# Attention over a graph's edges: the fifth chunk of slots of each group of sources becomes one chunk shared by four groups, scored once per block

## The chip, the cores and the metric

The kernel runs on one core of one Trainium2 chip. The metric is the device time of one launch in microseconds. Fourteen runs of the kernel before gave a median of 10038.4 us, from 10018.83 to 10051.82.

## The reference

The input is a graph of 10,000 nodes (512 features each) and 160,000 edges `src`, `dst` with eight attention biases per edge. Layer 0 is a mixture of four two-layer SAGE experts with a norm. Layer 1, which the change touches, is attention over the edges of each source:

```python
s = jnp.einsum('ehd,ehd->eh', q[src], k[dst]) / np.sqrt(D) + att_bias
m = jax.ops.segment_max(s, src, num_segments=n)
p = jnp.exp(s - m[src])
denom = jax.ops.segment_sum(p, src, num_segments=n)
alpha = p / jnp.where(denom[src] == 0, 1.0, denom[src])
agg = jax.ops.segment_sum(alpha[:, :, None] * v[dst], src, num_segments=n)
att = agg.reshape(n, C) @ Wo.T + bo
```

A residual, a norm and an MLP with `silu` (512 to 1024 to 512) follow, and a norm ends the layer.

## The kernel before

**Groups and slots.** The 10,112 padded nodes are 79 blocks of 128, and each block is four groups of 32 nodes (`W`=32, `NQ`=4), 316 groups in all (`NW`). A group has on average 506 edges. For layer 1 each group of sources owns five chunks (`CAP`=5) of 128 slots, 640 slots, in a table `sorted1` of ten floats per slot: the index of `dst`, the place of the source in its group, the eight biases. Empty slots carry an index out of bounds, which a gather skips. `fail` sends the launch to a slow general path if some group has more edges than slots.

**Three stages.** Stage 1 (to about 4000 us) and stage 2 (to about 7000 us) compute layer 0 and q, k, v, and TensorE is busy nearly throughout. Beside stage 1, `plan_src` works out each edge's slot on VectorE. It is a generator that `side(e, f)` drives from the loop of stage 1: four steps per call while it counts, then one. When it is done, `scatter_src` writes the edges to their slots, 128 per indirect DMA, 1250 DMAs: 28 per pair of blocks for the rest of stage 1, and seven per block in stage 2. Any that are left are issued at the end of stage 2.

**Stage 3** is the attention and the MLP, one loop iteration per group `w` (block `b`, `j = w % 4`). The order of instructions on TensorE (PE), VectorE (DVE), ScalarE (ACT) and GpSimd (POOL) is the order of the code. The attention of a group is spread over four iterations by the generator `weigh`. In iteration `w`:

1. `advance(EARLY)` issues MLP or output matmuls of earlier blocks (jobs `front`, `back`, `tail`) worth about 2.6 us of PE, with the ACT and DVE steps that belong to them.
2. `score(0)`: DVE multiplies two chunks of gathered k by the queries that PE has spread to the slots, in PSUM (`qe`, L1709). `score(1)` takes chunks 2 and 3, and `score(2)` the fifth chunk alone. `expand(w, g)` (L1695) makes `qe`: one matmul per chunk from the turned one-hots. There are two `qe` buffers, so `expand(w, 2)` waits for `score(0)`, `expand(w+1, 0)` for `score(1)`, `expand(w+1, 1)` for `score(2)`.
3. Between these, for group `w-1`: DVE takes a maximum (L1605), PE spreads it (L1607), DVE subtracts it (L1609), ACT takes the exponential (L1612), POOL and DVE multiply it into the one-hots (L1621). For `w-2`: PE adds up 80 small matmuls (L1635).
4. `pull(w+2)`: POOL issues the five gathers of k and v rows (L1476) into one of four buffers. The first is `ring`, which serves the groups with `j = 0`.
5. `turn_hots(w+2)`: PE turns five one-hots (L1485) into a PSUM bank named `turns`, and ACT copies them out (L1488). The bank `turns` holds the outputs of L1485, L1602 and L1607.
6. `advance(LATE)` issues job work worth about 2.4 us of PE. In it, ACT may have a Silu (L1545) of an MLP slice that PE has just made (L1543), or the normed rows (L1515), or a copy (L1527).
7. DVE sums the products over each head (L1736, five chunks at once), adds the bias (L1738), and takes the maximum over the chunks (L1600). PE turns that (L1602), and all later PE work stands behind it. Then come DVE's reciprocal (L1640, L1641) and ACT's scaling (L1644) for `w-2`.

The lines of step 7:

```python
s = dp.tile([P, CAP, H], F32, name="s")
nc.vector.tensor_reduce(s, kv[:, :, :D].rearrange("p c (h d) -> p c h d", h=H), axis=AX.X, op=ALU.add)
nc.vector.tensor_add(s, s, blocks[b][0][:, j * CAP:(j + 1) * CAP, 2:])
first = weigh(w, s)
next(first)                 # L1600: maximum over the chunks
next(first, 1)              # L1602: PE turns it
```

At `j = 1` the loop opens block `b+2`: it loads the slots and makes the one-hots (L1450 on DVE, L1452 on ACT).

Of the kernel before, what the change touches and what calls it, by code (L numbers as in the profile page):

```python
# [18 lines left out]
P = 128  # L19
# [606 lines left out]
NS = len(SEQ)  # L626
ET = mybir.EngineType
# [3 lines left out]
def fast(ctx: ExitStack, tc: tile.TileContext, a: dict, out: bass.AP, bad: bass.AP):  # L631

# [14 lines left out]
    NC = NW * CAP  # L647
# [16 lines left out]
    nc.gpsimd.iota(iota_w, pattern=[[1, W]], base=0, channel_multiplier=0,  # L664
                   allow_small_or_imprecise_dtypes=True)
# [230 lines left out]
    DIG = 1024.0  # L896
    SC = max(C, 2 * D)

    def plan_src(pool, ps):
        src_i = pool.tile([P, SC], I32, name="scan")[:, :C]  # L900
        nc.sync.dma_start(src_i, a["src"].rearrange("(p c) -> p c", c=C))
        pair = pool.tile([P, SC], BF16, name="pair")[:, :C]
        digit = pool.tile([P, C], BF16, name="digit")
        nc.vector.tensor_single_scalar(addr_i, src_i, 6, op=ALU.logical_shift_right)
        nc.vector.tensor_copy(pair, addr_i)
        nc.vector.tensor_scalar(addr_i, src_i, 5, 1, op0=ALU.logical_shift_right,
                                op1=ALU.bitwise_and)
        nc.vector.tensor_scalar(digit, addr_i, DIG - 1.0, 1.0, op0=ALU.mult, op1=ALU.add)
        yield
        count = pool.tile([P, NPR], F32, name="count")  # L910
        for b in range(NPR):
            m = pool.tile([P, C], BF16, name="m")
            nc.vector.scalar_tensor_tensor(m, pair, float(b), digit, op0=ALU.is_equal,  # L913
                                           op1=ALU.mult, accum_out=count[:, b:b + 1])
            yield
        num_i = pool.tile([P, NPR], I32, name="num_i")
        dig_i = pool.tile([P, NPR], I32, name="dig_i")
        nc.vector.tensor_copy(num_i, count)
        num = pool.tile([P, NPR, 2], F32, name="num")
        nc.vector.tensor_single_scalar(dig_i, num_i, 1023, op=ALU.bitwise_and)  # L920
        nc.vector.tensor_copy(num[:, :, 0], dig_i)
        nc.vector.tensor_single_scalar(dig_i, num_i, 10, op=ALU.logical_shift_right)
        nc.vector.tensor_copy(num[:, :, 1], dig_i)
        upper = pool.tile([P, P], F32, name="upper")
        nc.gpsimd.iota(upper, pattern=[[1, P]], base=0, channel_multiplier=-1,
                       allow_small_or_imprecise_dtypes=True)
        nc.vector.tensor_scalar(upper, upper, 0.0, None, op0=ALU.is_gt)
        flat = num.rearrange("p b q -> p (b q)")
        total = ps.tile([P, 512], F32, name="mm")
        nc.tensor.matmul(total[:, :NW], ones, flat, start=True, stop=True)  # L930
        top = pool.tile([P, 2], F32, name="top")
        nc.vector.tensor_reduce(top[:, 0:1], total[:, :NW], axis=AX.X, op=ALU.max)
        nc.vector.tensor_reduce(top[:, 1:2], total[:, :NW], axis=AX.X, op=ALU.add)
        nc.vector.tensor_scalar(fail[:, 1:2], top[:, 0:1], float(SL), None, op0=ALU.is_gt)
        nc.vector.tensor_scalar(fail[:, 2:3], top[:, 1:2], float(E), None, op0=ALU.not_equal)
        first = ps.tile([P, 512], F32, name="mm")
        nc.tensor.matmul(first[:, :NW], upper, flat, start=True, stop=True)
        two = first[:, :NW].rearrange("p (b q) -> p b q", q=2)
        nc.vector.tensor_copy(num, two)
        nc.vector.scalar_tensor_tensor(count, num[:, :, 1], DIG, num[:, :, 0],  # L940
                                       op0=ALU.mult, op1=ALU.add)
        nc.vector.memset(addr, 0.0)
        yield
        one = ones[:, 0:1].to_broadcast([P, C])
        for b in range(NPR):
            m = pool.tile([P, C], BF16, name="m")
            nc.vector.scalar_tensor_tensor(m, pair, float(b), digit, op0=ALU.is_equal,
                                           op1=ALU.mult)
            s = pool.tile([P, SC], F32, name="scan")[:, :C]
            nc.vector.tensor_tensor_scan(s, one, m, count[:, b:b + 1], op0=ALU.mult, op1=ALU.add)  # L950
            nc.vector.copy_predicated(addr, m.bitcast(mybir.dt.int16), s)
            yield

        nc.vector.tensor_sub(addr, addr, digit)
        rank = pool.tile([P, SC], I32, name="scan")[:, :C]
        nc.vector.tensor_copy(rank, addr)
        nc.vector.tensor_scalar(digit, digit, 1.0, 10.0 / (DIG - 1.0), op0=ALU.subtract,
                                op1=ALU.mult)
        nc.vector.tensor_copy(addr_i, digit)
        nc.vector.tensor_tensor(rank, rank, addr_i, op=ALU.logical_shift_right)  # L960
        yield
        nc.vector.tensor_scalar(digit, digit, 0.1, None, op0=ALU.mult)
        nc.vector.scalar_tensor_tensor(addr, pair, 2.0, digit, op0=ALU.mult, op1=ALU.add)
        nc.vector.tensor_scalar(addr, addr, float(CAP), None, op0=ALU.mult)
        part = pool.tile([P, C], I32, name="part")
        nc.vector.tensor_scalar(part, rank, 7, 7, op0=ALU.logical_shift_right,
                                op1=ALU.bitwise_and)
        nc.vector.tensor_add(addr, addr, part)
        nc.vector.tensor_single_scalar(part, rank, P - 1, op=ALU.bitwise_and)
        nc.vector.scalar_tensor_tensor(addr_i, part, float(NC), addr, op0=ALU.mult, op1=ALU.add)  # L970
        yield
# [3 lines left out]
    def scatter_src(pool):  # L975
# [3 lines left out]
        for c0 in range(0, C, GS):  # L979
# [6 lines left out]
            nc.vector.tensor_single_scalar(ends[:, 0, :n], ends[:, 0, :n], W - 1,  # L986
# [401 lines left out]
    with ExitStack() as p3:  # L1388
# [47 lines left out]
        kvb = [ring.rearrange("p (c v) -> p c v", c=CAP)]  # L1436
        kvb += [gp.tile([P, CAP, KVW], F32, name=f"kv{i}") for i in range(1, KB)]
# [6 lines left out]
        def open_block(b):  # L1444
            if b >= NB:
                return
            meta = dp.tile([P, BC, WP], F32, name="meta", bufs=3)
            nc.sync.dma_start(meta, slots1[:, b * BC:(b + 1) * BC, :])
            oh = dp.tile([P, BC, 3, W], BF16, name="oh", bufs=3)
            nc.vector.tensor_tensor(oh[:, :, 0, :], meta[:, :, 1:2].to_broadcast([P, BC, W]),  # L1450
                                    iota_w[:, None, :].to_broadcast([P, BC, W]), op=ALU.is_equal)
# [17 lines left out]

        def pull(w, cs):  # L1470

            if w >= NW:
                return
            b, j = divmod(w, NQ)
            for c in cs:
                nc.gpsimd.indirect_dma_start(  # L1476
                    out=kvb[w % KB][:, c, :], out_offset=None, in_=kv_all[:],
                    in_offset=bass.IndirectOffsetOnAxis(
                        ap=blocks[b][0].bitcast(I32)[:, j * CAP + c, 0:1], axis=0),
                    bounds_check=NP - 1, oob_is_err=False)  # L1480

        def turn_hots(w):
            b, j = divmod(w, NQ)
            for c in range(CAP):
                nc.tensor.transpose(hot_t[:3 * W, c, :], blocks[b][1][:, j * CAP + c, :, :]  # L1485
                                    .rearrange("p t n -> p (t n)"), identb)
            oh_t = dp.tile([3 * W, CAP, P], BF16, name="oh_t", bufs=4)
            nc.scalar.copy(oh_t, hot_t[:3 * W])  # L1488
            return oh_t
# [104 lines left out]
        def weigh(w, s):  # L1594
# [35 lines left out]
            kv = kvb[w % KB]  # L1630
            for c in range(CAP):
                for f in range(2):
                    for h in range(4):
                        v = D + (f * 4 + h) * VH
                        nc.tensor.matmul(acc[h * W:(h + 1) * W, f, :], ohp[:, c, f * 4 + h, :],  # L1635
                                         kv[:, c, v:v + VH], start=(c == 0 and f == 0),
# [38 lines left out]
        with tc.manual_schedule(engines={ET.PE, ET.DVE, ET.Activation, ET.Pool}):  # L1675
            for t in kvb[1:]:
# [3 lines left out]
            open_query(0)  # L1680
            for w in range(KB):
                pull(w, range(CAP))
            hots = {w: turn_hots(w) for w in range(2)}
            one, two, three = iter(()), iter(()), iter(())
            qe = {}

            GROUPS = [(0, 1), (2, 3), (4,)]
# [9 lines left out]

            expand(0, 0)
            expand(0, 1)
            EARLY, LATE = 2.6, 2.4  # L1700
            for w in range(NW + 3):
                b, j = divmod(w, NQ)
                kv = kvb[w % KB]

                def score(g):
                    if w < NW:
                        cs = GROUPS[g]
                        k = kv[:, cs[0]:cs[-1] + 1, :D]
                        nc.vector.tensor_tensor(k, qe.pop((w, g))[:, :len(cs), :], k, op=ALU.mult)  # L1709
# [6 lines left out]
                expand(w, 2)  # L1716
# [5 lines left out]
                expand(w + 1, 0)  # L1722
                score(2)
                next(one, 1)
                if w >= 2:
                    pull(w - 2 + KB, range(CAP))
# [4 lines left out]
                expand(w + 1, 1)  # L1731
                advance(LATE)
                first = iter(())
                if w < NW:
                    s = dp.tile([P, CAP, H], F32, name="s")
                    nc.vector.tensor_reduce(s, kv[:, :, :D].rearrange("p c (h d) -> p c h d", h=H),  # L1736
                                            axis=AX.X, op=ALU.add)
                    nc.vector.tensor_add(s, s, blocks[b][0][:, j * CAP:(j + 1) * CAP, 2:])  # L1738
# [68 lines left out]
```

## Time and profile before

| | |
|---|---|
| median of 14 runs | 10038.4 us |
| the profiled execution | 10027.07 us, of which the span is 10025.2 us |
| granted TensorE clock | 0.979 |
| busy share of the span | PE 94%, DVE 54%, POOL 71%, ACT 30% |
| loop of stage 3 | from 7038 us (first L1738) to 9928 us (last), 316 iterations |
| first and last scatter | 1488.8 us and 6888 us |

The profile is of one execution. A row of the view of groups gives a line, an engine, an operation, the tiles that it writes and reads, a count, busy time, the mean of one in nanoseconds, and the idle time of the engine before it with what ended it. The view of waits gives who waited for whom, with total, count and longest. The timeline gives start and duration of single instructions, and in brackets the idle time before them. A share over the whole span mixes three stages with different limits, so that stage 3 is read by itself.

### The profile page before, as it was taken

To read this page: it belongs to the slowest core of one execution; us is meant where nothing else is said; L and a number is where in the kernel's file an instruction comes from. 1 tells how busy PE (TensorE), PEld (TensorE's weight loads), DVE (VectorE), ACT (ScalarE), POOL (GpSimd) and SP (SyncE) were. 2 spreads that over 40 slices of the span, in tenths; PEclk is the share of its full clock that TensorE was granted. 3 is DMA by queue.
4 is the path that set the end of the run, shared out by engine and by line. 5 is a ranking of instruction groups with operands and counts; after the bars stand their busy time and mean duration, and the time that the engine had idled before them with its cause. 6 is when DMAs were issued, how large, how long until landed. Compare 5 with 4: busy or idle time off the path is not lost.

```text
span 10025.2 us, 169049 instructions
## 1 busy us (share of the span) xinstructions
PE 9441.3 (94%) x63574; PEld 5532.4 (55%) x63887; DVE 5378.4 (54%) x8205; ACT 2981.7 (30%) x5432; POOL 7126.4 (71%) x6972
## 2 busy tenths in 40 slices
PE   7999999999999998999999999999788888888888
PEld 4666666666666666333333333334455555555555
DVE  7898980000100003343343344333899999999996
ACT  1111111111111111111111111111466666666665
POOL 5566666777777774777777777775777777777774
PEclk9999999999999999999999999999799999999999
DMA  6544455455555543888888888886788888888884
GB/s 213 181 154 156 156 164 162 154 162 155 163 163 160 165 154 129 281 291 294 298 292 291 295 296 291 294 299 225 252 257 266 258 259 261 260 262 252 258 263 127
DMA packets 1110444, 2258.71 MB, mean 225 GB/s; under 512 B 284587, under 2 KB 534342, under 8 KB 1108848
## 3 DMA queue, kind: packets, MB, share of 16 engines
q0 software_dynamic: 622352, 1654.70, 51.6%
q1 hardware_dynamic: 479546, 579.42, 16.9%
q10 hardware_dynamic: 7718, 13.65, 0.4%
q8 instruction: 508, 8.32, 0.3%
q14 instruction: 320, 2.62, 0.1%
HBM read 2300.44 MB, written 380.18 MB: 267 GB/s over the span
## 4 chain that ended last, share of the span: by engine, by line
PE 68%; DVE 13%; DMA 9%; ACT 5%; issue 3%; POOL 1%; SPq 0%; POOLq 0%; ACTq 0%; DVEq 0%; another core or an unknown queue 0%
PE mm L1123 20%; PE mm L1314 11%; PE mm L1133 10%; PE mm L1276 6%; PE p_ag L1353 6%; DVE s L1736 3%; PE p_ag L1084 3%; DMA y<-y_tab,ix 3%; DMA ring<-kv_all,meta 3%; PE bank L1553 3%; DVE m L913 2%; PE bank L1503 2%; PE bank L1543 2%; DVE kv L1709 2%; ACT L1612 1%
## 5 line engine op out<-in xcount | busy, mean ns | idle before, releaser
L1059 POOL DMA_INDIRECT ring<-in_x_dram,idx_t x1580 | 1891.4, 1197 | 1006.4 <-PE p_ag L1084 559.8
L1123 PE MATMUL mm<-tt,big 128*128 128x256 f32 (+1 forms) x8960 | 1966.0, 378 | 0.0
L1123 PEld LDWEIGHTS mm<-tt,big 128*128 128x128 f32 x8960 | 1681.5, 190 | 290.5 <-issue 70.5
L993 POOL DMA_INDIRECT sorted<-pay,addr x1250 | 1270.7, 1017 | 385.4 <-issue 338.5
L1476 POOL DMA_INDIRECT kv<-kv_all,meta x1185 | 1214.6, 1025 | 330.1 <-issue 207.4
L1259 POOL DMA_INDIRECT y<-y_tab,ix x920 | 934.5, 1016 | 311.6 <-issue 189.8
L1314 PE MATMUL mm<-big,hb 128*128 128x512 f32 x2528 | 1145.9, 596 | 8.2
L1133 PE MATMUL mm<-wn,h 128*128 128x512 f32 x2528 | 1124.0, 597 | 0.0
L1125 ACT ACTIVATE h<-mm,bl 128x256 f32<-128x256 f32 (+1 forms) x640 | 301.3, 471 | 2126.8 <-PE mm L1123 2126.8
L1259 POOL DMA_INDIRECT ring<-y_tab,ix x660 | 684.8, 1038 | 292.1 <-issue 137.2
L1276 PE MATMUL mm<-big,z_t 128*128 128x512 f32 x1896 | 852.5, 592 | 0.8 <-ACT z_t L1269 0.7
L1133 PEld LDWEIGHTS mm<-wn,h 128*128 128x128 f32 x2528 | 468.6, 190 | 595.2 <-issue 594.2
L1314 PEld LDWEIGHTS mm<-big,hb 128*128 128x128 f32 x2528 | 468.7, 190 | 577.0 <-issue 513.3
L1709 DVE TENSOR_TENSOR kv<-qe,kv 128x1024 f32<-128x1024 f32 x711 | 722.2, 1037 | 89.2 <-PE qe L1695 83.2
L1543 PE MATMUL bank<-big,big 128*128 128x256 f32 (+1 forms) x2560 | 656.3, 402 | 87.7 <-ACT big L1545 83.6
L1736 DVE TENSOR_REDUCE s<-kv 128x40 f32<-128x2560 f32 x237 | 665.6, 2809 | 0.0
L1321 DVE SCALAR_TENSOR_TENSOR t<-mm,pick,t 128x512 f32<-128x512 f32 x474 | 334.1, 747 | 562.3 <-PE mm L1315 317.9
L891 DVE TENSOR_TENSOR oh<-loc_t,iota_w 128x640 f32<-128x640 bf16 x158 | 130.1, 824 | 923.3 <-PE p_ag L1084 872.9
L1553 PE MATMUL bank<-big,big 128*128 128x512 f32 x1264 | 613.0, 618 | 3.2 <-ACT big L1527 0.7
L1353 PE MATMUL p_ag<-y,oh 128*32 128x512 f32 x3680 | 567.2, 602 | 50.5 <-DMA y<-y_tab,ix 50.3
L1621 POOL TENSOR_TENSOR ohp<-oh,p 128x768 f32<-128x768 bf16 x316 | 466.7, 1477 | 207.3 <-ACT p L1612 206.2
L1543 PEld LDWEIGHTS bank<-big,big 128*128 128x128 f32 x2560 | 498.0, 202 | 209.2 <-ACT big L1545 111.3
(251 smaller groups left out, 13280.9 us busy)
## 6 DMA issues: line engine op xcount, KB each, us to landing
y_tab<-y SPq DMA_DIRECT2D x632, 256.0 KB
hb<-h_tab SPq DMA_DIRECT2D x316, 256.0 KB
h_tab<-h SPq DMA_DIRECT2D x156, 512.0 KB
kv_all<-kvt SPq DMA_DIRECT2D x79, 516.0 KB
xb<-in_x_dram SPq DMA_DIRECT2D x156, 256.0 KB
q_all<-q SPq DMA_DIRECT2D x79, 384.0 KB
q<-q_all SPq DMA_DIRECT2D x237, 128.0 KB
ring<-in_x_dram,idx_t POOLq DMA_INDIRECT x1580
```

Of the source, the lines that this page charges most:

```text
L993: inst = nc.gpsimd.indirect_dma_start(out=sorted1[:], out_offset=bass.IndirectOffsetOnAxis(ap=addr_i[:, c0 + c:c0 + c + 1], axis=0), in_=p ...
L1059: nc.gpsimd.indirect_dma_start(out=gbuf[i % GB], out_offset=None, in_=x, in_offset=bass.IndirectOffsetOnAxis(ap=window(idx_t, b)[:, j, c:c ...
L1123: nc.tensor.matmul(ph[:, :n], w[:, k, f * P:(f + 1) * P], tt[:, i, k, :n], start=(i + k == 0), stop=(i == 1 and k == KD - 1))
L1133: nc.tensor.matmul(py, h[:, k, i * P:(i + 1) * P], wn[e][:, k, :], start=(k == 0), stop=(k == KD - 1))
L1259: nc.gpsimd.indirect_dma_start(out=ybuf[i % YB], out_offset=None, in_=y_flat, in_offset=bass.IndirectOffsetOnAxis(ap=ahead[b][1][:, j, c:c ...
L1276: nc.tensor.matmul(po, z_t[:, k, :], wqkv[i][:, k, :], start=(k == 0), stop=False)
L1314: nc.tensor.matmul(pr, hb[:, k, :], wr[e][:, k, :], start=(k == 0), stop=False)
L1353: nc.tensor.matmul(p_ag[v][j * W:(j + 1) * W, :], oh[:, j * CAP + c, :], g[:, v * D:(v + 1) * D], start=(c == 0), stop=(c == CAP - 1))
L1476: nc.gpsimd.indirect_dma_start(out=kvb[w % KB][:, c, :], out_offset=None, in_=kv_all[:], in_offset=bass.IndirectOffsetOnAxis(ap=blocks[b][ ...
L1543: nc.tensor.matmul(ph, up(f, k), z_t[:, k, :m], start=(k == 0), stop=(k == KD - 1))
L1709: nc.vector.tensor_tensor(k, qe.pop((w, g))[:, :len(cs), :], k, op=ALU.mult)
L1736: nc.vector.tensor_reduce(s, kv[:, :, :D].rearrange("p c (h d) -> p c h d", h=H), axis=AX.X, op=ALU.add)
```

## The change

Each group keeps four chunks of its own. What a group has past 512 edges goes to one chunk of 128 slots per block, shared by its four groups. The slots per block are 17 chunks for 20 (`SBC`), and `fail` is now set if a block's shared chunk would overflow. In stage 3:

- POOL issues four gathers per group and one per block (`pull_over`, at `j = 0` for the next block, into one of three buffers `kvo`).
- `score(2)` and `expand(w, 2)` are gone. Per block, at `j = 3`, PE makes the queries of the next block's shared chunk with four matmuls into one PSUM region (`expand_over`) and DVE multiplies, sums and adds the bias (`score_over`), giving `s_over`.
- The one-hots of the shared chunk still exist per group, and are made from the source's place in its block of 128 (`iota_q`). PE turns four per group, and four per block at `j = 2` (`over_t`), behind `advance(LATE)`. ACT copies those out there too.
- In step 7 the sum and the bias cover four chunks. The fifth column of `s` is copied from `s_over` by ACT.
- The matmuls with v (L1635) still run over five chunks per group, the fifth being the shared one.

`plan_src` has a longer end: more DVE instructions over the 1250 edges of each partition, in 15 steps where there were 3.

```diff
+SC_W = CAP - 1
+SBC = NQ * SC_W + 1
-    NC = NW * CAP
+    NC = NB * SBC
...
+        for c in range(2, SC_W):
+            v.scalar_tensor_tensor(digit, u, float(c * P), digit, op0=ALU.is_ge, op1=ALU.add)
+        madd(u, digit, -float(P), u)
+        madd(pair, pair, SC_W, digit)
+        yield
...
-            nc.vector.tensor_tensor(oh[:, :, 0, :], meta[:, :, 1:2].to_broadcast([P, BC, W]),
-                                    iota_w[:, None, :].to_broadcast([P, BC, W]), op=ALU.is_equal)
+            nc.vector.tensor_tensor(mine[:, :, :SC_W, :],
+                                    loc[:, :, :, None].to_broadcast([P, NQ, SC_W, W]),
+                                    iota_q[:, :, None, :].to_broadcast([P, NQ, SC_W, W]),
+                                    op=ALU.is_equal)
+            nc.vector.tensor_scalar(mine[:, :, SC_W, :], iota_q, meta[:, SBC - 1, 1:2], None,
+                                    op0=ALU.is_equal)
...
-            GROUPS = [(0, 1), (2, 3), (4,)]
+            GROUPS = [(0, 1), (2, 3)]
...
+            def expand_over(b):
+                if b < NB:
+                    qe[b] = px.tile([P, 2, D], F32, name="qe")
+                    for j in range(NQ):
+                        nc.tensor.matmul(qe[b][:, 0, :], over_t[b][:, j, :], queries[b][:, j, :],
+                                         start=(j == 0), stop=(j == NQ - 1))
+            def score_over(b):
+                if b < NB:
+                    k = kvo[b % 3][:, :D]
+                    nc.vector.tensor_tensor(k, qe.pop(b)[:, 0, :], k, op=ALU.mult)
+                    s = s_over[b] = dp.tile([P, H], F32, name="s_over")
+                    nc.vector.tensor_reduce(s, k.rearrange("p (h d) -> p h d", h=H),
+                                            axis=AX.X, op=ALU.add)
+                    nc.vector.tensor_add(s, s, blocks[b][0][:, SBC - 1, 2:])
...
                 next(two, 1)
-                expand(w, 2)
+                if last:
+                    expand_over(b + 1)
+                else:
+                    expand(w + 1, 0)
                 advance(0)
                 next(one, 1)
                 score(1)
                 next(one, 1)
                 next(two, 1)
-                expand(w + 1, 0)
-                score(2)
+                expand(w + 1, 0 if last else 1)
+                if last:
+                    score_over(b + 1)
                 next(one, 1)
                 if w >= 2:
-                    pull(w - 2 + KB, range(CAP))
+                    pull(w - 2 + KB, range(SC_W))
+                    if j == 0:
+                        pull_over(b + 1)
                 advance(0)
                 next(three, 1)
                 if w + 2 < NW:
                     hots[w + 2] = turn_hots(w + 2)
-                expand(w + 1, 1)
+                if last:
+                    expand(w + 1, 1)
                 advance(LATE)
+                if j == 2 and b + 1 < NB:
+                    over_t[b + 1] = turned(b + 1, range(SC_W, BC, CAP), "over_t", 2)
                 first = iter(())
                 if w < NW:
                     s = dp.tile([P, CAP, H], F32, name="s")
-                    nc.vector.tensor_reduce(s, kv[:, :, :D].rearrange("p c (h d) -> p c h d", h=H),
+                    nc.scalar.copy(s[:, SC_W, :], s_over[b])
+                    nc.vector.tensor_reduce(s[:, :SC_W, :],
+                                            kv[:, :, :D].rearrange("p c (h d) -> p c h d", h=H),
                                             axis=AX.X, op=ALU.add)
-                    nc.vector.tensor_add(s, s, blocks[b][0][:, j * CAP:(j + 1) * CAP, 2:])
+                    nc.vector.tensor_add(s[:, :SC_W, :], s[:, :SC_W, :],
+                                         blocks[b][0][:, j * SC_W:(j + 1) * SC_W, 2:])
                     first = weigh(w, s)
                     next(first)
```

## The prediction

> **What bounds the kernel now.** I read the page first: PE is busy 94% of the span, but in the last quarter, the loop of attention, every engine is. So I read that loop alone, in 2000 us from its middle, in the view of busy time by window:
>
> ```profile
> core 0: us, PE busy (x) PEld busy (x) DVE busy (x) ACT busy (x) POOL busy (x), PEclk, DMA share, GB/s
> 7600.00:9600.00 2000.00, 1780.06 (x23717) 1171.59 (x23815) 1843.46 (x2992) 1268.92 (x2309) 1558.38 (x1575) 0.97 0.82 259
> ```
>
> The stretch holds 217 iterations (the count of L1738), so 9.2 us each, of which DVE is busy 8.5 and PE 8.2. Both are nearly full: what leaves DVE can bring PE's idle time at most. That idle time is in the view of waits, same stretch:
>
> ```profile
> PE turns L1602 <- DVE den L1640: 130.4, 89, 2.3
> PE bank L1543 <- ACT big L1545: 50.8, 72, 1.2
> DVE kv L1709 <- PE qe L1695: 59.9, 39, 2.5
> DVE ring L1709 <- DMA ring<-kv_all,meta: 45.0, 33, 2.7
> PE qe L1695 <- DVE ring L1709: 5.2, 9, 1.1
> ```
>
> PE waits for DVE mainly at L1602, step 7 (the row names L1640, the DVE instruction behind L1600, which PE waits for), in 89 of 217 iterations; and for a Silu (L1545), in about three iterations of eight, since an MLP runs once per two blocks. The groups of the stretch, by form, give the prices:
>
> ```profile
> L1736 DVE TENSOR_REDUCE s<-kv 128x40 f32<-128x2560 f32 x164 | 460.6, 2808 | 0.0
> L1709 DVE TENSOR_TENSOR kv<-qe,kv 128x512 f32<-128x512 f32 x164 | 112.2, 684 | 60.6 <-PE qe L1695 59.9 <-PE turns L1607 0.6
> L1738 DVE TENSOR_TENSOR s<-s,meta 128x40 f32<-128x40 f32 x217 | 102.3, 472 | 7.5
> L1605 DVE TENSOR_REDUCE top<-turns 128x1 f32<-128x128 f32 x217 | 61.2, 282 | 0.0
> L1488 ACT COPY oh_t<-turns 96x640 bf16<-96x640 bf16 x217 | 148.6, 685 | 0.4
> L1612 ACT ACTIVATE p<-s 128x40 f32<-128x40 f32 x217 | 51.3, 237 | 125.5 <-DVE s L1609 123.3
> ```
>
> Last the timeline at three ends of an iteration: one with j = 2, one with a Silu in the late job work, one where PE waits longest.
>
> ```profile
> 8338.47 2.84 PE L1503 MATMUL bank<-big,att_t 128*128 128x512 f32 x6 [0.50 <-ACT att_t L1647]
> 8340.75 0.23 DVE L1600 TENSOR_REDUCE wide<-s 128x8 f32<-128x40 f32 x1
> 8341.15 0.28 PE L1602 MATMUL turns<-ident,wide 128*128 128x128 f32 x1
> ...
> 8349.77 0.22 DVE L1600 TENSOR_REDUCE wide<-s 128x8 f32<-128x40 f32 x1
> 8350.14 0.30 PE L1602 MATMUL turns<-ident,wide 128*128 128x128 f32 x1 [1.20 <-DVE den L1640]
> 8350.16 0.47 ACT L1545 ACTIVATE big<-bank,b 128x256 f32<-128x256 f32 x1
> 8350.69 0.70 PE L1543 MATMUL bank<-big,big 128*128 128x256 f32 x2 [0.25 <-ACT big L1545]
> ...
> 8318.24 1.98 PE L1553 MATMUL bank<-big,big 128*128 128x512 f32 x4
> 8322.27 0.30 PE L1602 MATMUL turns<-ident,wide 128*128 128x128 f32 x1 [2.04 <-DVE den L1640]
> ```
>
> In the first PE waits for nothing: L1600 is done when the job work ends. In the second L1602 runs beside the Silu, and the next MLP matmul starts 0.06 us after the Silu. In the third PE loses 2.04 us to DVE.
>
> **What DVE gains.** Per iteration `score(2)` goes, 0.68 us. L1605 and L1736 give 1.04 ns per element ((2808 - 282) / 2432), so four chunks take 2.28 us for 2.81: 0.53 saved. Per block come the multiply (0.68), a sum over 512 (0.68) and an add (0.20, the shortest L1738), 1.56 us, or 0.39 per iteration; the second one-hot instruction adds some 0.03. Net 0.8 us of 8.5, 250 us over 316 iterations. But only PE's waits for DVE can shorten the loop: 137 us in the stretch with the smaller rows, 199 us in the whole loop, were all of it to go.
>
> L1738 reads two tiles in SBUF. Its mean is 0.47 us and its shortest 0.20. The Trainium skill (GPSIMD Engine Reference, Specifications) says that VectorE instructions with two SBUF inputs contend with GpSimd for the SBUF interfaces. By that, L1738 would be drawn out until POOL's L1621 is through wherever it comes too early, and part of the 0.53 us would be lost in it: 0.27 less gain per iteration if half of them are so. The sum below does not use it.
>
> **What the change adds to the path.** The fifth column of `s` is now written by ACT, and L1600 reads it. So L1600, L1602 and all PE work behind L1602 stand behind whatever ACT has queued ahead of that copy. I count per eight iterations (two blocks; 39.5 such in the loop).
>
> (a) j = 2, twice. Behind the late job work, where PE had no wait, come four transposes, an ACT copy of 512 (0.57 us: 685 ns for 640, 246 for the 128 of L1647), the column copy (0.24, as L1612), L1600 (0.23), and the hand to PE (0.15, from the rows above, and some 0.05 in all for the other hands). Each waits for the one before: 1.2 us in which PE has nothing. Bounds 0.8 (copies half overlapped) to 1.3. Twice: +2.4 (1.6 to 2.6).
>
> (b) A Silu in the late work, three times. Before, L1543 followed the Silu by 0.06 us. Now the column copy (0.24), L1600 (0.23), the hand (0.15) and L1602 (about 0.11 before the next matmul may enter) come between: 0.7, less 0.1 for the smaller L1488 on ACT. +1.8; of this 0.5 returns in the one iteration where ACT's chain began with an exponential that waited for `score(2)`. +1.3 (0 to 2.1).
>
> (c) j = 3, twice. DVE has 1.56 in place of 0.68, less 0.53: 0.35 us more, and starts late, since at j = 2 it stood waiting for ACT with its whole queue (`score(0)`, L1621 and L1605 of the next iteration) behind L1600. Following the timeline from such a start, L1600 comes about 0.55 us behind the end of PE's late work. +1.1 (0 to 2.8).
>
> (d) Gains: the iteration with 2.04 us of wait has 1.2 us less of DVE work ahead of L1602 (0.68 + 0.53): -1.2 (-0.5 to -2.0). PE's waits at L1695: -0.2. The other L1602 waits are mostly ahead of a Silu that PE would wait for anyway. DVE's wait for L1695 (59.9 us) falls to one iteration of four, but that is in the DVE time that PE no longer needs.
>
> Sum: 2.4 + 1.3 + 1.1 - 1.4 = +3.4 us per eight, times 39.5: +134 us. With all ends low, 1.6 + 0 + 0 - 2.2 = -0.6, or -24 us; with all high, 2.6 + 2.1 + 2.8 - 0.5 = 7.0, or +277. As not all ends meet, +40 to +230.
>
> A second reason for (a): `turns` is one PSUM bank. In the trace L1543 waits for a Silu that reads the other half of its bank (the row of 50.8 us). The Trainium skill (PSUM — Partial Sum Buffer, PSUM bank collisions raise a hardware error) has the rule to guard PSUM by bank and quadrant, not by address. By it, L1602 would wait for the copy of `over_t` even without the column copy, and (a) would keep at least its 0.57 + 0.15 of 1.2.
>
> **What costs nothing, and its cover.** PE's matmuls and transposes per block stay 20 and 20. POOL loses 0.75 gathers per iteration, 1.0 us of 7.2 busy; nobody waits for POOL but through the 45.0 us at `ring`, in bounds (d). The bytes gathered are the same, as empty slots are skipped. The end of `plan_src` takes 12 steps more; the steps of stage 1 come 14 per 97 us, so scatters begin 83 us later and, counted through the code, 556 for 533 remain for stage 2, which takes 553. They end at its last block, 3 behind it, about 4 us on POOL, which from 6958 to 7014 us has no gather to issue. The some 40 us more of DVE work are under PE, which from 250 to 3800 us is busy 3539 of 3550; without that cover they would cost at most those 40. Counted from the inputs, the fullest block needs 121 of its 128 shared slots, so the general path stays unused.
>
> **Rivals.**
>
> A, faster. The column copy is not last: PE's late work ends so much ahead of DVE that ACT is through before L1738. It decides where PE leads DVE by over 1.2 us (j = 2) or 0.6 (Silu). For it: at 8320.22 (8318.24 + 1.98) PE was 2.0 us ahead of L1602. Against: no lead at 8341. Then (a) to (c) shrink and DVE's relief works: between nothing and 199 us, I take 110: 9928 us. Chance 0.20.
>
> B, much slower. The column and the other four are written by two engines into one tile, and L1736 itself waits for the copy, so that 2.28 us more stand behind ACT in the five iterations of (a) and (b): 5 x 2.5 x 39.5 = 490 us on top: 10,660. For it: L1543's wait on the other half of a bank. Against: POOL and DVE write halves of `ohp` (L1621), and DVE's has no idle time ahead of it. Chance 0.05.
>
> C, no change: (a) to (c) near their low ends, about 2.4, with (d) at 2.2: within 20 us. Chance 0.09.
>
> **How the numbers follow.** The sum stands on the profiled execution, 10027 us (span 10025.2 and 1.9 around it); the median of the runs, 10038, is 11 us above. 10027 + 134 + 11 = 10,172 us, chance 0.66, its own range 10,078 to 10,268. To leave out no more than 2 in 10, half of A is taken in below; B and a little more stay out above: 9940 to 10,270. About 0.2%, 20 us, is what a measurement can tell here from no change: slower 0.71, same 0.09, faster 0.20.
>
> **What would show it.** Right: the loop's DVE busy time per iteration falls to near 7.7 us while the period rises by 0.3 to 0.5; L1600 waits for ACT, most at j = 2 with over 1.5 us; PE's idle at L1602 there is near 1.2 us; stages 1 and 2 end as before, within 10 us. Wrong: L1600 finds the column ready, or the idle at L1602 falls below the 130 us of before; then A holds, and the loop is shorter. B: L1736 itself shows idle time for ACT.

## The result, and the profile after

The changed kernel takes 10174.94 us (median of 6 runs), beside 10040.63 us for the kernel before (28 runs): a ratio of 1.0135, 95% interval 1.0125 to 1.0145. It is slower by 134 us. The experiments ran in three jobs on three chips, and on the first two of these every kernel, the one before too, took some 10% longer, so that times are compared only within a job, by their ratio to the kernel before beside them.

The profiled execution has a span of 10181.1 us for 10025.2. The first L1684 (L1602 before) starts at 7044.6 us for 7038.9, so stages 1 and 2 cost 6 us. The other 150 us lie in the loop of attention: 9.66 us per iteration for 9.17. Line numbers have moved: L1852 is the sum over each head (L1736), L1855 the bias add (L1738), L1851 ACT's column copy, L1682 the maximum over the chunks (L1600), L1684 its turn on PE (L1602), L1625 and L1627 the MLP matmul and Silu (L1543, L1545), L1703 the weighted one-hots (L1621), L1585 the output matmul (L1503).

Busy time by window, the same 2000 us of the loop:

```profile
core 0: us, PE busy (x) PEld busy (x) DVE busy (x) ACT busy (x) POOL busy (x), PEclk, DMA share, GB/s
7600.00:9600.00 2000.00, 1698.83 (x22381) 1109.61 (x22486) 1635.98 (x2836) 1235.77 (x2448) 1345.15 (x1339) 0.97 0.77 245
```

They now hold 206 iterations for 217. Every engine is busy for less of the time, DVE most clearly (82% for 92%). When all are idler and the loop is longer, a wait has come in. The view of waits names it:

```profile
DVE wide L1682 <- ACT s L1851: 275.1, 129, 3.8
PE turns L1684 <- DVE wide L1682: 235.9, 175, 3.4
DVE s L1691 <- PE turns L1689: 46.5, 84, 1.7
PE bank L1585 <- ACT att_t L1729: 41.9, 51, 1.2
```

The first row did not exist. DVE waits for ACT's copy of eight numbers per partition in 129 iterations of 206, on average 2.1 us. The second was 130.4 us. The groups by form show that the removed work did go:

```profile
L1852 DVE TENSOR_REDUCE s<-kv 128x32 f32<-128x2048 f32 x155 | 352.5, 2274 | 0.0
L1855 DVE TENSOR_TENSOR s<-s,meta 128x32 f32<-128x32 f32 x206 | 141.3, 686 | 7.1
L1682 DVE TENSOR_REDUCE wide<-s 128x8 f32<-128x40 f32 x206 | 45.9, 223 | 283.0 <-ACT s L1851 275.1
L1851 ACT COPY s<-s_over 128x8 f32<-128x8 f32 x206 | 39.7, 193 | 0.0
```

The copy itself takes 0.19 us. What stands ahead of it on ACT is seen in the timeline. First an iteration with j = 2:

```profile
8408.13 2.84 PE L1585 MATMUL bank<-big,att_t 128*128 128x512 f32 x6 [0.94 <-ACT att_t L1729]
8409.03 0.29 DVE L1855 TENSOR_TENSOR s<-s,meta 128x32 f32<-128x32 f32 x1
8410.81 0.39 PE L1567 MATMUL turns<-identb,oh 128*96 128x128 bf16 x4
8411.24 0.58 ACT L1570 COPY over_t<-turns 96x512 bf16<-96x512 bf16 x1 [2.67 <-PE turns L1567]
8411.72 0.20 ACT L1851 COPY s<-s_over 128x8 f32<-128x8 f32 x1
8411.95 0.22 DVE L1682 TENSOR_REDUCE wide<-s 128x8 f32<-128x40 f32 x1 [2.63 <-ACT s L1851]
8412.23 0.33 PE L1684 MATMUL turns<-ident,wide 128*128 128x128 f32 x1 [1.03 <-DVE wide L1682]
```

DVE is ready at 8409.32 and then stands for 2.63 us: PE finishes its late job work and turns the shared chunk's one-hots, ACT copies them out, ACT copies the column. PE meanwhile has nothing for 1.03 us. Next an iteration with a Silu in the late work:

```profile
8420.48 1.28 ACT L1627 ACT_TABLE_LOAD   x1
8421.27 0.19 DVE L1855 TENSOR_TENSOR s<-s,meta 128x32 f32<-128x32 f32 x1
8421.77 0.47 ACT L1627 ACTIVATE big<-bank,b 128x256 f32<-128x256 f32 x1
8422.14 0.19 ACT L1851 COPY s<-s_over 128x8 f32<-128x8 f32 x1
8422.36 0.22 DVE L1682 TENSOR_REDUCE wide<-s 128x8 f32<-128x40 f32 x1 [0.90 <-ACT s L1851]
8422.64 0.33 PE L1684 MATMUL turns<-ident,wide 128*128 128x128 f32 x1 [1.99 <-DVE wide L1682]
8422.80 2.27 PE L1625 MATMUL bank<-big,big 128*128 128x256 f32 x6
```

From the end of the Silu (8422.24) to the next MLP matmul are 0.56 us, where there were 0.06. The Silu is late because ACT first loads a table for it, 1.28 us. The kernel before has the same load ahead of its Silu (from 8348.86), so the load is no cost of the change, but L1682 now waits for it too. And the iteration where PE waited 2.04 us for DVE:

```profile
8390.04 1.94 PE L1635 MATMUL bank<-big,big 128*128 128x512 f32 x4
8392.68 0.33 PE L1684 MATMUL turns<-ident,wide 128*128 128x128 f32 x1 [0.70 <-DVE wide L1682]
```

Here the change does what it says: 0.70 us are left.

### The profile page after: what moved, and what is told of

The parts are those of the page before. It is cut to its first block, busy times and chain, and to the rows that moved or that the text cites. A ratio compares the mean times of both kernels' runs of the same rounds, so it can differ in the third digit from the quotient of the medians.

```text
span 10181.1 us, 168601 instructions
## 1 busy us (share of the span) xinstructions
PE 9464.8 (93%) x63574; PEld 5530.1 (54%) x63887; DVE 5245.1 (52%) x8244; ACT 3030.2 (30%) x5827; POOL 6931.3 (68%) x6736
## 4 chain that ended last, share of the span: by engine, by line
PE 69%; DVE 11%; ACT 9%; DMA 6%; issue 3%; POOL 1%; ACTq 0%; DVEq 0%; POOLq 0%; SPq 0%
PE mm L1187 20%; PE mm L1378 11%; PE mm L1197 10%; PE mm L1340 6%; PE p_ag L1417 6%; PE p_ag L1148 3%; DMA y<-y_tab,ix 3%; PE bank L1585 3%; PE bank L1635 3%; DVE m L927 2%; DVE s L1852 2%; ACT L1694 2%; PE bank L1625 2%; ACT L1627 2%; DMA ring<-y_tab,ix 1%
## 5 line engine op out<-in xcount | busy, mean ns | idle before, releaser
L1543 POOL DMA_INDIRECT kv<-kv_all,meta x948 | 994.0, 1049 | 260.5 <-issue 181.7
L1703 POOL TENSOR_TENSOR ohp<-oh,p 128x768 f32<-128x768 bf16 x316 | 466.8, 1477 | 646.5 <-ACT p L1694 646.4
L1625 PE MATMUL bank<-big,big 128*128 128x256 f32 (+1 forms) x2560 | 662.8, 406 | 15.9 <-ACT big L1627 11.9
L1441 ACT ACTIVATE t<-t,gsel 128x512 f32<-128x512 f32 x158 | 109.2, 722 | 1638.6 <-DVE t L1439 1638.5
L1635 PE MATMUL bank<-big,big 128*128 128x512 f32 x1264 | 589.9, 595 | 3.3 <-ACT big L1609 0.7
L1340 PEld LDWEIGHTS mm<-big,z_t 128*128 128x128 f32 x1896 | 360.1, 190 | 425.8 <-issue 415.8
L1814 DVE TENSOR_TENSOR kv<-qe,kv 128x1024 f32<-128x1024 f32 x474 | 575.0, 1213 | 5.1 <-DMA kv<-kv_all,meta 4.5
```

The costliest lines, as they stand in the source:

```text
L1340: nc.tensor.matmul(po, z_t[:, k, :], wqkv[i][:, k, :], start=(k == 0), stop=False)
L1543: nc.gpsimd.indirect_dma_start(out=to, out_offset=None, in_=kv_all[:], in_offset=bass.IndirectOffsetOnAxis(ap=blocks[b][0].bitcast(I32)[:, ...
L1625: nc.tensor.matmul(ph, up(f, k), z_t[:, k, :m], start=(k == 0), stop=(k == KD - 1))
L1635: nc.tensor.matmul(po, hid[:, k, i * P:(i + 1) * P], w2[k // KD][:, k % KD, :], start=(k == 0), stop=False)
L1814: nc.vector.tensor_tensor(k, qe.pop((w, g)), k, op=ALU.mult)
```

## The experiments

Two theories. **Q**, the queue: L1682 and all that follows stand behind ACT's late work, because the column copy does. **W**, the work: the time is that of the change's own instructions, wherever they stand.

| run | ratio to the kernel before | 95% interval | job |
|---|---|---|---|
| changed kernel | 1.0135 | 1.0125 to 1.0145 | first comparison |
| e1, column copy ahead | 0.998 | 0.9953 to 1.0008 | 1 |
| e2, turns ahead | 0.9982 | 0.9961 to 1.0003 | 1 |
| e3, both ahead | 0.9887 | 0.9852 to 0.9922 | 1 |
| e4, before with PE linked | 0.9995 | 0.9965 to 1.0025 | 1 |
| changed kernel again | 1.0087 | 1.0057 to 1.0117 | 2 |
| e3 again | 0.9917 | 0.9891 to 0.9944 | 2 |
| e4 again | 1.0022 | 0.9991 to 1.0053 | 2 |
| e5, shared scores at j = 2 | 0.9912 | 0.988 to 0.9944 | 2 |
| e6, before with DVE linked | 1.0114 | 1.0097 to 1.0131 | 3 |
| e7, no weights on POOL | 0.9992 | 0.9981 to 1.0002 | 3 |
| e8, two chunks on POOL | 0.996 | 0.9946 to 0.9974 | 3 |
| e3, third time | 0.9975 | 0.9965 to 0.9985 | 3 |

The kernel before had medians of 11071.18, 11042.22 and 10029.39 us in the three jobs.

**e1: the column copy issued ahead of the late job work.**

```diff
+                if w < NW:
+                    s = dp.tile([P, CAP, H], F32, name="s")
+                    nc.scalar.copy(s[:, SC_W, :], s_over[b])
                 advance(LATE)
...
                 if w < NW:
-                    s = dp.tile([P, CAP, H], F32, name="s")
-                    nc.scalar.copy(s[:, SC_W, :], s_over[b])
```

> The changed kernel with the column copy of s issued on ACT ahead of the late job work instead of behind it; same work, another place in ACT's queue. Theory Q (the copies wait in ACT's queue, and L1682, L1684 and PE behind them): the 275 us in which L1682 waits for the column in the 2000 us from 7600 fall below 40, the three Silu iterations of eight give back some 0.6 us each and the two with j = 2 some 0.25 each, as L1684 still waits for the copy of over_t out of the same bank: -2.3 us per eight, some 10,085 us (10,050 to 10,120). Theory W (the time is the change's own work: 1.56 us of the shared chunk on DVE at j = 3, moved transposes, the bias add drawn out beside POOL; places on ACT do not matter): 10,160 to 10,190.

Measured 0.998 of the kernel before, where the changed kernel stands at 1.0087 on a chip like it: 1.1% less, where Q put 0.9% (0.5 to 1.2). Waits of DVE and PE in e1, 2000 us from 8400, where its loop runs on this chip:

```profile
DVE wide L1682 <- ACT s L1847: 65.6, 58, 1.7
PE turns L1684 <- ACT over_t L1570: 25.5, 38, 0.7
```

L1682's wait for the column is 66 us, against 322.8 in the changed kernel in job 2, so not quite below the 40 of the expectation. The second row is new and answers a side question. DVE is ready, and PE still waits up to 0.7 us at L1684 for ACT to copy `over_t` out of another part of the bank `turns`.

**e2: the shared chunk's turns ahead.** They now stand behind L1689, so that the 80 small matmuls cover ACT's copy.

```diff
                 score(1)
                 next(one, 1)
+                if j == 2 and b + 1 < NB:
+                    over_t[b + 1] = turned(b + 1, range(SC_W, BC, CAP), "over_t", 2)
...
                 advance(LATE)
-                if j == 2 and b + 1 < NB:
-                    over_t[b + 1] = turned(b + 1, range(SC_W, BC, CAP), "over_t", 2)
```

> The changed kernel with the four transposes of the shared chunk's one-hots and their ACT copy issued at j = 2 behind L1689, ahead of the 80 small matmuls, instead of behind the late job work; the column copy stays. Theory Q: PE's 1.03 us without work ahead of L1684 at j = 2 go, twice per eight, and DVE is earlier by over 1.5 us in the iterations with j = 3, where some 0.3 to 0.7 us more of PE's idle time goes: -2.1 to -2.8 us per eight, some 10,080 us (10,055 to 10,110). Theory W: the same transposes and copies are made, 10,160 to 10,190.

Measured 0.9982, again 1.0% below the changed kernel. PE's idle time ahead of L1684 at j = 2, 1.03 us in the changed kernel on both kinds of chip, is 0.00. The sum of eight periods is 77.2 us, against 80.0 in the changed kernel in job 2: -2.8 us.

**e3: both moves.** The two diffs together.

> Both moves. Theory Q: the two add, -4.4 us per eight, some 10,000 us (9,950 to 10,040), so faster than the kernel before, because DVE's saving of some 0.5 to 0.8 us per iteration then meets PE's remaining waits for DVE; L1682 has no idle time for ACT. Theory W: 10,160 to 10,190.

Measured 0.9887. The changed kernel was then run on such a chip too, with e3 once more:

> The changed kernel itself, run beside its relatives. On the chip of the first experiments every kernel took 10% more, with gathers that landed later, so a base for ratios on the same chip is wanted. Both theories: ratio to the kernel before 1.0135 where DMA is as in the first comparison; less, 1.00 to 1.01, where late gathers leave ACT's waits some cover.

> Both copies ahead of the late job work, as in e3. Theory Q: ratio to the changed kernel 0.977 to 0.987 wherever it runs (-4.4 us per eight iterations less what late gathers hide); the period of the loop 9.1 us or less where DMA is quick. Theory W: 0.998 to 1.002 of the changed kernel.

Measured 1.0087 and 0.9917: e3 is 0.983 of the changed kernel, between Q's bounds. L1682 still waits for the column, for 69.2 us in 2000 (40.4 in the third run below), where Q had it without any wait. In the third job, on a chip on which the kernel before takes its usual time:

> Both copies ahead of the late job work, a third time, beside the runs above. Theory Q: ratio to the kernel before 0.975 to 0.995, so faster than both kernels on whichever chip. Theory W: 1.008 to 1.014.

Measured 10001.0 us against 10029.39, ratio 0.9975 (0.9965 to 0.9985). W is out: the same instructions, in other places of the same queues, are faster than the kernel before. e3 beats both kernels. Its period there is 9.15 us, a little over the 9.1 of the expectation.

**e4: the kernel before with PE linked to ACT.** Nothing of the change but a wait of L1602 for ACT's queue.

```diff
+        nil = wp.tile([P, H], F32, name="nil")
+        nc.vector.memset(nil, 0.0)
...
                     s = dp.tile([P, CAP, H], F32, name="s")
+                    nc.scalar.copy(wide[w % 2][:, H:2 * H], nil)
```

> The kernel before with nothing of the change but the link: ACT copies eight zeros into spare columns of the tile that L1602 turns, at the place where the change copies its column, so that PE's turn waits for ACT's queue (DVE does not). Theory Q: no over_t here, so only the three Silu iterations of eight lose, 0.4 to 0.8 us each: +50 to +95 us on 10,040, some 10,105. Theory W: no measurable change, 10,030 to 10,060.

> The kernel before with the link alone. Theory Q: +50 to +95 us, ratio to the kernel before 1.005 to 1.010, where DMA is quick; none where the gathers end last. Theory W: 1.000 everywhere.

Measured 0.9995 and 1.0022, both with 1 in their interval: a miss for Q on the chips it ran on. PE does wait for the copy there, 39.5 us in 2000 in the second run, but the time shows no cost. It was not run on a chip of the usual speed.

**e6: the kernel before with DVE linked.** The same link one step earlier, as the change has it.

```diff
-                    s = dp.tile([P, CAP, H], F32, name="s")
+                    s = dp.tile([P, CAP + 1, H], F32, name="s")
+                    nc.scalar.copy(s[:, CAP, :], nil)
...
             nc.vector.tensor_reduce(wd[:, :H], s.rearrange("p c h -> p h c"), axis=AX.X, op=ALU.max)
+            s = s[:, :CAP, :]
```

> The kernel before with the link as the change has it, and nothing else of the change: s has a sixth column that ACT fills with -1e9 behind the late job work, and L1600's maximum reads it, so that DVE's whole queue stands behind ACT's. Between this and the run where PE alone was linked lies the part of DVE's queue. Theory Q, as first written (PE's wait at L1602 is the price): as with PE alone, within 30 us of the kernel before. Theory Q2 (the price comes by way of DVE: while it stands, the scores, maxima and weights of the next iteration are late and PE meets them late): slower by 1.2 to 2.2 us per eight iterations, ratio 1.004 to 1.009. Theory W: 1.000.

Measured 1.0114: +119 us by the medians, from one ACT copy per iteration and the order that it imposes. Waits of e6 in 2000 us of the loop:

```profile
DVE wide L1602 <- ACT s L1739: 124.6, 77, 2.5
PE turns L1605 <- DVE wide L1602: 195.0, 99, 3.3
PE turns L1605 <- DVE den L1643: 59.2, 35, 3.2
```

DVE waits in 77 of 208 iterations, the three Silu iterations of eight. PE's waits at the turn grow from 130.4 to 254.2 us. They grow in iterations without a Silu too: at j = 1 in the second block of the pair, PE's idle time ahead of the turn is 2.09 us where it was 0.02. Per eight iterations the period grows by 3.2 us. In the three Silu iterations PE's idle time at the turn grows by 3.4 us, less 2.0 of waits for the Silu that are gone: 1.4 us. The other large part, 2.1 us, is that wait at j = 1 in the second block. So a large part of the price lies away from the link, as Q2 has it, and the price is higher than Q2 put it. How the lateness gets to that place is not shown: at j = 2 and 3 in between PE does not wait. What PE's link alone would cost on a chip of this speed was not run, so the share of DVE's queue is not measured.

**e5: the shared chunk's scores one iteration earlier.** To test step (c).

```diff
-                last = j == NQ - 1
+                last = j == NQ - 2
...
-                if j == 2 and b + 1 < NB:
+                if j == 1 and b + 1 < NB:
                     over_t[b + 1] = turned(b + 1, range(SC_W, BC, CAP), "over_t", 2)
...
+                if j == 0:
+                    open_query(b + 1)
                 if j == 1:
                     open_block(b + 2)
-                    open_query(b + 1)
```

> Both copies ahead, and the shared chunk's scores made at j = 2 instead of j = 3 (its turns at j = 1, its queries loaded one iteration sooner). It tests step (c), DVE's 1.56 us at j = 3. Theory Q with (c): in the iteration with j = 3 and a Silu, PE's idle time ahead of L1684, 1.17 us in e3, falls below 0.5 and the sum of the period over eight iterations by 0.6 to 1.5 us, 25 to 60 us on the launch. Rival (DVE's place is free, PE is full at j = 3): no difference from e3, within 15 us.

Measured 0.9912 beside e3's 0.9917. PE's idle time at j = 3 with a Silu falls from 1.17 to 0.72 us, the way (c) has it, though not below 0.5, but the periods at j = 2 grow by 1.25 us each, and the time stays within 4 us. The rival fits better: once ACT's waits are gone, it makes no difference that shows at which of the two places the 1.56 us stand. The intervals, some 30 us to each side, are too wide to exclude the low end of (c), 25 us.

**e7 and e8: who draws out the bias add.** L1855 takes 0.19 us at its shortest and 0.69 on average. In the changed kernel 173 of its 316 instances are longer than 0.25 us, and 167 of these end within 0.12 us after POOL's L1703.

```diff
-        OWN = 2
+        OWN = CAP
...
-            weighted(nc.gpsimd, OWN, CAP)
             nc.gpsimd.tensor_tensor(over, over, far, op=ALU.add)
```

> Both copies ahead, and all five chunks of the weighted one-hots (L1703) made on DVE, none on POOL. It tests whether the bias add (L1855 in the changed kernel, 0.69 us mean, shortest 0.19) is drawn out by POOL's L1703. If so, its mean falls to 0.20 to 0.22 with no long ones but beside POOL's other tensor instructions; if it is drawn out by something else (the gathers POOL issues, the sum ahead of it), it stays above 0.5. The time is no measure here: DVE has 0.8 us more and 0.5 less per iteration, within 1% of e3 either way.

> Both copies ahead, and POOL weights two chunks instead of three, DVE three instead of two. If POOL's L1703 draws out the bias add, that falls by 0.3 to 0.5 us, DVE's L1703 rises by 0.27, and the loop gains nothing or up to 0.5 us per eight iterations: within 20 us of e3. If the bias add ends last in the Silu iterations, 20 to 50 us faster than e3.

e8 is e3 with `OWN = 3`. The bias add by form in e3's third run, in e8 and in e7, in this order (it is L1856 in the first two):

```profile
L1856 DVE TENSOR_TENSOR s<-s,meta 128x32 f32<-128x32 f32 x218 | 141.6, 649 | 7.5
```

```profile
L1856 DVE TENSOR_TENSOR s<-s,meta 128x32 f32<-128x32 f32 x218 | 109.3, 502 | 7.5
```

```profile
L1855 DVE TENSOR_TENSOR s<-s,meta 128x32 f32<-128x32 f32 x217 | 42.7, 197 | 7.5
```

Without L1703 on POOL, the add is near its shortest on average; the 16 of 316 that are still longer than 0.25 us all end with another tensor instruction of POOL. With two chunks of it for three it is in between, though it falls by 0.15 us and not the 0.3 to 0.5 expected. In time e8 (9996.32 us) cannot be told from e3, and e7, with more work on DVE, has the kernel before in its interval.

## Why the prediction was right

The forecast was 10,172 us, and 10174.94 came. The sum gave +3.4 us per eight iterations; the eight periods of the loop add up to 77.74 us for 73.68, +4.1. (The two profiled executions lie 156 us apart, the medians 134.) The mechanism was right in (a), (b) and (d), and wrong in (c). The table has means over iterations 20 to 295, by the iteration's place among eight (j in brackets; the Silu iterations are 7, 0 and 1):

| us | 0 (0) | 1 (1) | 2 (2) | 3 (3) | 4 (0) | 5 (1) | 6 (2) | 7 (3) |
|---|---|---|---|---|---|---|---|---|
| PE idle ahead of the turn (L1602, L1684), before | 1.27 | 0.24 | 0.00 | 0.02 | 2.02 | 0.02 | 0.00 | 1.22 |
| changed kernel | 2.60 | 1.22 | 1.03 | 0.08 | 0.71 | 0.85 | 1.03 | 1.99 |
| e3, third run | 0.56 | 0.37 | 0.00 | 0.10 | 0.70 | 0.84 | 0.00 | 1.22 |
| e6 | 2.56 | 1.49 | 0.00 | 0.00 | 1.51 | 2.09 | 0.07 | 2.09 |
| bias add (L1738, L1855), before | 1.04 | 1.00 | 0.44 | 0.22 | 0.20 | 0.44 | 0.20 | 0.23 |
| changed kernel | 0.50 | 1.20 | 0.97 | 0.19 | 0.19 | 2.01 | 0.30 | 0.19 |
| e3, third run | 0.19 | 1.59 | 0.69 | 0.19 | 0.19 | 2.00 | 0.19 | 0.19 |

- (a), j = 2: 1.03 us of idle time twice, +2.1 for +2.4. The chain of hands was as drawn, and the hands cost a little less. e2 takes it away. DVE's own wait there is 2.63 us, over 1.5 as said, but at place 0 it is longer still, 2.9.
- (b), the Silu iterations: idle time ahead of L1684 grows from 1.22, 1.27 and 0.24 to 1.99, 2.60 and 1.22, +3.1. The waits of the MLP matmul for the Silu go, -1.8 per eight by these rows of the two pages (behind the last bar stands the idle time ahead of it, over the whole span):

```profile
L1543 PE MATMUL bank<-big,big 128*128 128x256 f32 (+1 forms) x2560 | 656.3, 402 | 87.7 <-ACT big L1545 83.6
L1625 PE MATMUL bank<-big,big 128*128 128x256 f32 (+1 forms) x2560 | 662.8, 406 | 15.9 <-ACT big L1627 11.9
```

Net +1.3, the figure of the prediction. e1 and e3 take the growth at the turn away. In the iteration shown above the direct part is 0.5 us. How the price divides between PE's link and DVE's was not separated on a chip of this speed (e4, e6).
- (c), j = 3, put at +1.1, did not come: without a Silu PE's idle time there is 0.08 us for 0.02, and with one its growth is already in (b) and goes with ACT's waits (1.22 us in e3's third run, as before the change). Two waits that the sum did not have came instead. One is +0.8 at place 5. It is not the lateness of DVE that (c) follows from j = 2, as it is as long in e3's third run, where DVE finds the column ready at j = 2. The trace puts it to the bias add, which takes 2.01 us at that place for 0.44 and stands right ahead of L1682:

```profile
8398.15 1.29 POOL L1598 TENSOR_TENSOR x<-x,x 128x512 f32<-128x512 f32 x1
8398.87 2.05 DVE L1855 TENSOR_TENSOR s<-s,meta 128x32 f32<-128x32 f32 x1
8399.37 1.49 POOL L1703 TENSOR_TENSOR ohp<-oh,p 128x768 f32<-128x768 bf16 x1
8401.02 0.22 DVE L1682 TENSOR_REDUCE wide<-s 128x8 f32<-128x40 f32 x1
8401.30 0.33 PE L1684 MATMUL turns<-ident,wide 128*128 128x128 f32 x1 [0.85 <-DVE wide L1682]
```

The add is held while two tensor instructions of POOL run, one behind the other: so in 37 of the 39 iterations at that place, and in one of 39 in the kernel before. Counted from the turn before, the add now starts 0.8 us sooner and POOL's pair 0.65 us later, so that it falls into the first of them. The prediction named this loss and left it out of its sum. No run tests it alone: e7 shortens the add to 0.19 us, but gives DVE 0.8 us more work, and PE's idle time there is 1.06 us. The other wait is +0.7 in PE's wait for `att_t` (41.9 us in 206 iterations at L1585, for the row below in 217). It too is as large in e3's third run (44.2 us in 218); its cause is open.

```profile
PE bank L1503 <- ACT att_t L1647: 24.9, 53, 0.8
```

- (d), the gain: 2.02 us to 0.71, -1.3 for -1.2; PE's waits for DVE at L1695 give 0.1 more, for 0.2.
- The total: the four terms as measured make +2.1, the two waits +1.5, and PE's own busy time grows from 8.20 to 8.25 us per iteration, +0.35 per eight, together 4.0 of the 4.1. That the forecast came within 3 us is luck: the +1.1 of (c) did not come, and waits that the sum did not have took its place.
- DVE's saving, 0.8 us per iteration in the prediction, is 0.55 (8.49 to 7.94 busy), as L1855 grew from 0.47 to 0.69 us on average. This is the loss that the Trainium skill's rule on SBUF interfaces (GPSIMD Engine Reference, Specifications) let expect, put at 0.27 if half the iterations were so. e7 shows the cause. The profile after was said to show 7.7 us of DVE per iteration; it shows 7.9.
- The second reason for (a), drawn from the rule to guard PSUM by bank and quadrant (PSUM — Partial Sum Buffer, PSUM bank collisions raise a hardware error): e1's row, PE's turn waiting for ACT's copy of `over_t` while DVE waits for nothing, agrees, with 0.67 us at j = 2.
- The covers held: stages 1 and 2 end 6 us later, scatters begin 77 us later (83 predicted) and end at 6976 us, ahead of the first gather of stage 3.

Of the rivals, A needed DVE to find the column ready, and it does in 77 iterations of 206. B would have shown L1852 idle for ACT: it shows 0.0. B's price was also reckoned with 2.5 us per iteration where its text has 2.28, which makes 450 us and not 490.

Where did the expected gain go, when the waits are taken away? In e3 DVE is as relieved as in the changed kernel (7.94 us), yet the kernel gains 0.25%. Waits of PE in e3, 2000 us of the loop in the third job:

```profile
PE turns L1684 <- DVE wide L1682: 79.8, 93, 1.3
PE bank L1625 <- ACT big L1627: 72.6, 73, 1.9
PE bank L1585 <- ACT att_t L1729: 44.2, 54, 1.3
PE turns L1684 <- DVE den L1722: 22.1, 30, 1.3
```

PE's wait at the turn falls from 130.4 to 101.9 us, and its waits for ACT rise from 75.7 (50.8 and 24.9) to 116.8. What DVE no longer holds up, ACT does. PE is busy 8.1 us of 9.15 per iteration, so that 1.05 us is the most that is left to win.

## What to carry to other kernels

Before a cheap instruction is given to an engine with time to spare, look at what stands ahead of it in that engine's queue at that place, and at what will stand behind its result on the other engines: here 0.19 us of ACT per iteration cost 119 us when put into the kernel before, and moving it and the shared chunk's turns with their 0.58 us copy in the code turned +1.35% into -0.25%. When two engines are nearly full and wait for each other, time saved on one is worth only the other's waits for it, and a wait put into one engine's queue can show up again iterations later, where nothing was changed (2.09 us for 0.02 in e6). It pays to tabulate waits by the iteration's place: a term that looks confirmed in the total can have come out of another place, for another reason.

## What the runs showed that I had not expected

- A short DVE instruction with two inputs in SBUF is drawn out to the end of a POOL tensor instruction that runs beside it, or of two that follow each other: the bias add takes 0.19 to 2.58 us in the changed kernel, and 0.197 on average when POOL's 1.47 us L1703 is gone. POOL's gathers hardly ever do this: the 78 adds of the changed kernel that began beside a gather alone took 0.193 us on average and 0.24 at most, and in the kernel before one of 118 such adds was held (3.41 us). At place 5 the add so takes up 1.6 us more than before, where DVE had been relieved.
- The size of e6: one copy and one dependency, +1.14% (0.97% to 1.31%), against at most 0.9% expected.
- On two of the chips, PE waits at the 80 small matmuls (L1717) with no releaser that the profile shows: 107.5 us in 2000 in e3 there, and no such row in e3's third run. What it waits for is open.
